# Householder steps of an on-chip eigensolver: z and y from one product, the rank-two update on 65 rows, and layer-0 work in 256-column pieces

## The chip, the cores and the metric

One core of one Trainium2 chip runs the whole program in one launch. The metric is device time in microseconds (us), the median of several runs. Engines are named as the profile names them: PE (TensorE, matrix products), DVE (VectorE), ACT (ScalarE), POOL (GpSimd), SP (SyncE, which issues the DMAs).

## What is computed

The input x is (128, 64, 256) in float32, with an adjacency matrix of 64 nodes. Four layers follow one another, each a layer norm, a ReLU, a graph layer, and an addition to x. Two of them matter here:

```python
# layer 0
agg = einsum('nm,bmd->bnd', A_hat, h)              # mix of the 64 nodes
h0  = relu(batchnorm(agg @ W1.T + b1))             # 256 -> 512
x   = x + batchnorm(h0 @ W2.T + b2)                # 512 -> 256
# layer 1
L_norm = d_inv_sqrt[:, None] * (diag(deg) - A) * d_inv_sqrt[None, :]
_, U = linalg.eigh(L_norm)                         # 64 x 64
agg = einsum('mn,bnd->bmd', U.T, h)
x   = x + einsum('nm,bmd->bnd', U, relu(agg @ W1 + b1) @ W2 + b2)
```

Layer 2 runs small LSTMs over windows, layer 3 is a graph attention. The eigenvectors of layer 1 depend only on the adjacency matrix, so they can be computed beside layer 0.

## The kernel before

The eigenvectors come from a chain of small, dependent steps; layer 0 is large and independent of them. `eigenvectors` (L1593) lays both into one order per engine. A `Plan` (L843) holds a model of time: each step has an engine, a `busy` time, a `ready` time after which its readers may start, and its needs. `chain` (L883) places a step of the eigensolver at once; before it does so, `fill` (L870) takes waiting steps of layer 0 (those given to `beside`, L889) into the gap ahead of it, as long as they end before the chain step's inputs are due plus a slack of the engine: 0.6 us for PE (T), 0.3 for ACT (S) and DVE (V). At most five PSUM banks of layer-0 results are open at a time. `emit` sorts all by planned time, and a helper (L799, the line that the profile gives for nearly every instruction) ties each instruction to the one before it on its engine. So the order on every engine is fixed when the program is built; nothing is reordered on the chip.

**The chain.** `tridiagonal` (L1003) reduces the 64x64 matrix `A` in 62 Householder steps, c = 63 down to 2, each by `householder` (L1041). A step holds the current row in every one of 64 partitions (`x`). Its norm comes from a Square with accumulation (ACT, `f_ja`), a Sqrt (`s0`), a reciprocal and a product on DVE (`r`, `tt`), and with the sign (`q`) gives the off-diagonal element `nb`. A small fix sets the reflector's entry, with `OA` holding a copy (on ACT) of an element of x. `KAP` is the reciprocal that scales the reflector, `uk` the scaled row (ACT). On PE two products make the rows z (one row of `A`, by a column of the identity) and y (a column of `A` times `A`), each broadcast to all partitions; ACT copies z from PSUM. DVE makes `uA` = z nb + y, a dot product `c2`, the row `v`, and from them the next step's row x in two instructions, ahead of the matrix itself. PE adds the two outer products of `uk` and `v` (contraction over one row), and DVE adds the result to `A`. Each row x is also sent to the matrix V by a DMA on SP; the row tiles x have eight buffers.

**The layer-0 work beside it.** 16 blocks of 512 rows. `hidden_block` (L1807): ReLU on ACT, per half of the features four 128x128 products with the mixing matrix into one PSUM bank (tile `ps`, one planned step), a copy on ACT, then 8 products of 512 columns, with statistics on DVE and a copy on ACT. `features0` (L1848), after batch-norm constants are known: ReLUs, 8 products of 512 columns per block, an output copy with a sum and a Square with a sum on ACT (tile `sums`). In float32 each product runs as two passes of the array.

**What follows.** After the last step the reflectors and the eigenvector computation proper (`fast.vectors`) run, with the rest of the planned layer-0 work. A verdict, `f_k_bad`, is summed by a PE product, and every engine reads it and branches over a slow path (L1617 and L1618). Then the constants of the second batch norm (`bn_b`, `bn_v`, `bn_r`, `bn_sh`) and the layer-1 inputs (`big`, ACT) are made.

Of the kernel before, what the change touches and what calls it, by code (L numbers as in the profile page):

```python
# [8 lines left out]
F32 = mybir.dt.float32  # L9
I32 = mybir.dt.int32  # L10
AF = mybir.ActivationFunctionType
ALU = mybir.AluOpType
# [772 lines left out]
GRID = 64  # L785

# [56 lines left out]
class Plan:  # L843
# [55 lines left out]

    def rest(self):  # L900

        while any(self.queue.values()):
            for e in self.queue:
                self.fill(e, 1e9)
# [8 lines left out]
class Fast:  # L913
# [31 lines left out]
    def sum(self, out, a, s, b, op0, op1=ALU.mult, name="junk"):  # L945

        w = a.shape[-1]
        j = self.t(f"{name}{a.shape[0]}", a.shape[0], 64)
        self.o.stt(j[:, 0:w], a, s, b, op0, op1, acc=out)
# [3 lines left out]
    def constants(self):  # L953
# [6 lines left out]
        self.P = t("P", 64, 1)  # L960
        iota(self.P[:], [[0, 1]], 0, 1)
# [21 lines left out]
        o.ts(self.low[:], self.J[:64, :], self.P[:], ALU.is_lt)  # L983
# [3 lines left out]
        o.copy(pi[:], self.P[:])  # L987
# [15 lines left out]
    def tridiagonal(self, S, made, plan):  # L1003

        o, nc, t = self.o, self.nc, self.t
        ident = self.k.ident
        A = self.A = t("A", 64, 64)
        m = t("SR", 64, 64)
        NB, OA, KAP, V = t("NB", 64, 64), t("OA", 64, 64, 2), t("KAP", 64, 64), t("V", 64, 64)
        nc.vector.memset(OA[:], 1.0)  # L1010
        for x in (KAP, NB, V):
            nc.vector.memset(x[:], 0.0)
        s0, r, tt, q, c2 = (t("h_" + x, 64, 1) for x in "s0 r t q c2".split())
        ja = t("ja", 64, 64)
        bc = lambda c, n=64: c.to_broadcast([n, 64])
        now = {}
        go = plan.chain

        def keep(name, a, b):
            now[name] = self.mm((a, b))  # L1020

        d = go("T", lambda: keep("p", S, self.JR[:]), [made], 0.3, 0.5)
        d = go("V", lambda: o.copy(m[:], now["p"][:]), [d], 0.15, 0.28)
        d = go("T", lambda: keep("p", self.JR[:], m[:]), [d], 0.3, 0.5)
        rest = go("V", lambda: o.copy(A[:], now["p"][:]), [d], 0.15, 0.28)
        d = go("T", lambda: keep("p", bc(ident[:64, 63:64]), A[:]), [rest], 0.3, 0.5)

        def first():
            x = now["x"] = self.rows.tile([64, 65], F32, name="f_x", bufs=8)
            o.copy(x[:, 0:63], now["p"][:, 0:63])  # L1030

        def square(w):
            x = now["x"]
            self.act(ja[:, 0:w], x[:, 0:w], AF.Square, accum_out=x[:, w:w + 1])

        row = go("V", first, [d], 0.15, 0.28)
        h = go("S", lambda: square(63), [row], 0.34, 0.42)
        for c in range(63, 1, -1):
            row, h, rest = self.householder(c, now, go, row, h, rest, (s0, r, tt, q, c2), square)

    def householder(self, c, now, go, row, h, rest, scalars, square):  # L1041

        o, nc, t = self.o, self.nc, self.t
        ident = self.k.ident
        A, NB, OA, KAP, V = self.A, t("NB", 64, 64), t("OA", 64, 64, 2), t("KAP", 64, 64), t("V", 64, 64)
        s0, r, tt, q, c2 = scalars
        bc = lambda a, n=64: a.to_broadcast([n, 64])
        x = lambda a, b: now["x"][:, a:b]
        nb = NB[:, c - 1:c]
        e, w = 0.001 * c, c - 1  # L1050

        def zy():
            now["zp"] = self.ps.tile([64, 64], F32, name="fps")
            nc.tensor.matmul(now["zp"][:, 0:c], bc(ident[0:c, c - 1:c], c), A[0:c, 0:c], start=True, stop=True)
            now["yp"] = self.ps.tile([64, 64], F32, name="fps")
            nc.tensor.matmul(now["yp"][:, 0:c], bc(A[0:c, c:c + 1], c), A[0:c, 0:c], start=True, stop=True)

        def row_z():
            now["z"] = self.rows.tile([64, 64], F32, name="f_z")
            self.act(now["z"][:, 0:c], now["zp"][:, 0:c], AF.Copy)  # L1060

        def row_uk():

            nc.sync.dma_start(V[c:c + 1, 0:c], now["x"][0:1, 0:c])
            now["uk"] = self.rows.tile([64, 64], F32, name="f_uk")
            self.act(now["uk"][:, 0:c], x(0, c), AF.Copy, scale=KAP[:, c:c + 1])

        def row_uA():
            now["uA"] = self.rows.tile([64, 64], F32, name="f_uA")
            o.stt(now["uA"][:, 0:c], now["z"][:, 0:c], nb, now["yp"][:, 0:c], ALU.mult, ALU.add)  # L1070

        def row_v():
            now["v"] = self.rows.tile([64, 64], F32, name="f_v")
            o.stt(now["v"][:, 0:c], x(0, c), c2[:], now["uA"][:, 0:c], ALU.mult, ALU.subtract)

        def outer():
            uk, v = now["uk"], now["v"]
            p = now["p"] = self.ps.tile([64, 64], F32, name="fps")
            nc.tensor.matmul(p[0:c, 0:c], uk[0:1, 0:c], v[0:1, 0:c], start=True, stop=False)
            nc.tensor.matmul(p[0:c, 0:c], v[0:1, 0:c], uk[0:1, 0:c], start=False, stop=True)  # L1080

        def row_x():
            now["x"] = self.rows.tile([64, 65], F32, name="f_x", bufs=8)
            o.stt(x(0, w), now["uk"][:, 0:w], now["v"][:, w:c], now["z"][:, 0:w], ALU.mult, ALU.add)

        z = go("T", zy, [rest], 0.34, 0.42)
        sq = go("S", lambda: self.act(s0[:], x(c, c + 1), AF.Sqrt), [h], 0.13, 0.23)
        oa = go("S", lambda: self.act(OA[:, c, 1:2], x(c - 1, c), AF.Copy), [row], 0.12, 0.22)
        zs = go("S", row_z, [z], 0.15, 0.26 + e)  # L1090
        sg = go("V", lambda: o.ts(q[:], x(c - 1, c), **halve(0)), [row])
        d = go("V", lambda: o.recip(r[:], s0[:]), [sq])
        d = go("V", lambda: o.stt(tt[:], r[:], x(c, c + 1), s0[:], ALU.mult, ALU.add), [d, h])
        b = go("V", lambda: o.mul(nb, q[:], tt[:]), [d, sg])
        d = go("V", lambda: o.stt(x(c - 1, c + 1), OA[:, c, :], nb, x(c - 1, c + 1), ALU.mult, ALU.add), [b, oa])
        d = go("V", lambda: o.recip(KAP[:, c:c + 1], x(c, c + 1)), [d])
        uk = go("S", row_uk, [d], 0.16, 0.32 + e)
        d = go("V", row_uA, [zs, b, z], 0.12 + e, 0.25 + e)
        d = go("V", lambda: self.sum(c2[:], now["uA"][:, 0:c], 0.5, now["uk"][:, 0:c], ALU.mult), [uk, d],
               0.2 + e, 0.28 + e)  # L1100
        v = go("V", row_v, [d], 0.15 + e, 0.26 + e)
        p = go("T", outer, [v], 0.25, 0.45)
        if c > 2:
            row = go("V", row_x, [v], 0.15 + e, 0.22 + e)
            row = go("V", lambda: o.stt(x(0, w), now["v"][:, 0:w], now["uk"][:, w:c], x(0, w), ALU.mult, ALU.add),
                     [row], 0.15 + e, 0.25 + e)
            h = go("S", lambda: square(w), [row], 0.28 + e, 0.36 + e)
        rest = go("V", lambda: o.add(A[0:c, 0:c], A[0:c, 0:c], now["p"][0:c, 0:c]), [p], 0.12 + e, 0.22 + e)
        return row, h, rest

    def reflectors(self):
# [8 lines left out]
        self.sum(kc[:], self.KAPs[:], 1.0, ident, ALU.mult)  # L1120
# [22 lines left out]
    def scale(self):  # L1143

        o, nc, t = self.o, self.nc, self.t
        NB, A = t("NB", 64, 64), self.A
        self.KAPs = t("KAP", 64, 64)
        DM, NE = t("DM", 64, 64), t("NE", 64, 64)
        o.mul(DM[:], A[:], self.k.ident[:64, :64])
        pe = self.mm((self.k.ident[:64, 1:2].to_broadcast([64, 64]), A[:]))  # L1150
# [315 lines left out]
class Kernel:  # L1466
# [126 lines left out]
    def eigenvectors(self):  # L1593
# [3 lines left out]
        with ExitStack() as ex:  # L1597
            fast = Fast(self.tc, ex, self)
            fast.constants()
            plan = Plan(dict(T=0.6, S=0.3, V=0.3), 5)  # L1600
# [206 lines left out]
    def hidden_block(self, i, r, m, plan, needs, used):  # L1807
# [9 lines left out]
        def mix(dc):  # L1817
            p = now["m", dc] = psum.tile([P, BT], F32, name="ps")
            for j in range(TPB):
                self.mm(p[:, j * P:(j + 1) * P], now["h"][:, j, dc * P:(dc + 1) * P], self.BDH[:])  # L1820

        def product(hc, kc):
            if kc == 0:
                now["p", hc] = psum.tile([P, BT], F32, name="ps")
            self.mm(now["p", hc][:], W1[:, kc, hc * P:(hc + 1) * P], now["z"][:, 2 + kc, :], kc == 0, kc == 1)
# [3 lines left out]
        for dc in range(2):  # L1829
            bank = []  # L1830
            x = beside("T", lambda dc=dc: mix(dc), h, 0.98, 1.1, bank)
# [4 lines left out]
        for hc in range(4):  # L1836
            bank = []
            x = beside("T", lambda hc=hc: product(hc, 0), mixed, 0.86, 0.9, bank)
            x = beside("T", lambda hc=hc: product(hc, 1), [x], 0.86, 1.0)
# [8 lines left out]
    def features0(self, plan, made, used):  # L1848
# [21 lines left out]
        for i in range(NB):  # L1870
# [15 lines left out]
            def product(oc, kc, i=i, now=now):  # L1886
                if kc == 0 and ("p", oc) not in now:
                    now["p", oc] = psum.tile([P, BT], F32, name="ps")
                self.mm(now["p", oc][:], W2[:, kc, oc * P:(oc + 1) * P], now["z"][:, kc, :], kc == 0, kc == 3)
# [11 lines left out]
            for oc in range(2):  # L1901
# [4 lines left out]
                for kc in range(4):  # L1906
                    x = beside("T", lambda oc=oc, kc=kc, f=product: f(oc, kc), [z[kc]] + ([x] if x else []), 0.86, 1.0,
                               None if kc or x else bank)
# [878 lines left out]
```

## Time and profile before

| | |
|---|---|
| median of 3 runs | 2329.3 us (2326.33 to 2331.57) |
| profiled execution, span | 2325.1 us |
| first outer product of the chain | 14.87 us |
| last update of A | 272.2 us |
| verdict product (f_k_bad) on PE | 364.35 us |
| PE goes on after the branch | 370.16 us |
| layer-1 inputs begin on ACT | 372.03 us |
| mean interval of outer products (61 of them) | 4.2 us |

The profile is one execution on the chip. Its page gives the busy time of each engine; the busy time can be had for any stretch of the span, and a timeline lists instructions one after the other with start, length, engine, operation, the output and the inputs by tile names, the array's rows and columns in use (128*128 for a full product) and the shape. Consecutive alike instructions are merged (x6: six passes). PE's passes overlap, so the distance between two starts says more than the length of one. In brackets stand idle time ahead of an instruction and what ended it. Of the span the first 372 us, less than a sixth, hold all that the change touches; layers 1 to 3 after it are the same in both kernels.

### The profile page before, as it was taken

Reading aid. Unit: us, or ns where it says so; the run is one execution under the profiler, and the core shown is the slowest. Engines: PE = TensorE matmul, PEld = TensorE weight load, DVE = VectorE, ACT = ScalarE, POOL = GpSimd, SP = SyncE. Lnnn points to the kernel's source line nnn. Section 1 sums busy time; section 2 is a strip of 40 time slices with the busy share of each in tenths; the row PEclk is TensorE's granted clock in tenths of the full one; section 3 lists DMA queues with packets and bytes.
Section 4 is the critical chain, followed back from the end, with each engine's and each line's share of the span. In section 5 each row is a group of like instructions: output and inputs, shape, how many; then the busy total and the mean of one; then the engine's idle time right before and its main releaser. Section 6 shows DMA issues by size and latency. Waiting matters only on the chain.

```text
span 2325.1 us, 32725 instructions
## 1 busy us (share of the span) xinstructions
PE 2283.6 (98%) x12169; PEld 1633.1 (70%) x12169; DVE 1629.3 (70%) x4054; ACT 1139.5 (49%) x2483; POOL 3.0 (0%) x26
## 2 busy tenths in 40 slices
PE   7999998999999999999999999999999999999999
PEld 4554445676777788888999998888885544554544
DVE  8887676888447777666767676559756686766667
ACT  5765865754436654433444444336435544444321
POOL 0000000000000000000000000000000000000000
PEclk9999999999999999999999999999999999999999
DMA  5000211230000000001000002000010000000001
GB/s 171 1 1 26 65 56 30 71 83 19 1 37 0 1 19 1 1 1 37 1 1 1 1 1 73 1 1 17 1 46 28 1 5 15 15 19 14 14 24 46
DMA packets 61065, 54.81 MB, mean 24 GB/s; under 512 B 15203, under 2 KB 58724, under 8 KB 60900
## 3 DMA queue, kind: packets, MB, share of 16 engines
q1 hardware_dynamic: 60900, 52.66, 7.4%
q8 instruction: 97, 1.59, 0.3%
q14 instruction: 68, 0.56, 0.1%
HBM read 35.86 MB, written 16.78 MB: 23 GB/s over the span
## 4 chain that ended last, share of the span: by engine, by line
PE 79%; DVE 3%; issue 1%; ACT 1%; DMA 0%; SPq 0%; ACTq 0%; DVEq 0%
PE ps L799 69%; PE acc L799 5%; PE pt L799 4%; PE pe L799 1%; PE y L799 1%; DVE aw L799 1%; DVE X L799 1%; DVE sm_m L799 0%; DVE XV L799 0%; ACT ls_g L799 0%; ACT h L799 0%; DVE ls_g L799 0%; ACT big L799 0%; DVE ls_t L799 0%; DVE sm_e L799 0%
## 5 line engine op out<-in xcount | busy, mean ns | idle before, releaser
L799 ACT ACTIVATE ls_g<-ls_g,ls_b 128x512 f32<-128x512 f32 (+4 forms) x472 | 243.1, 565 | 151.4 <-DVE ls_g L799 149.6
L799 ACT ACTIVATE ls_g<-ps,ls_b 128x256 f32<-128x256 f32 (+3 forms) x268 | 115.5, 470 | 330.9 <-PE ps L799 327.7
L799 PE MATMUL ps<-z,w 128*128 128x512 f32 x512 | 254.9, 621 | 0.9 <-ACT z L799 0.9
L799 PE MATMUL ps<-big,X 128*128 128x176 f32 (+3 forms) x848 | 212.7, 366 | 0.1
L799 DVE TENSOR_TENSOR ls_g<-ls_z,ps 128x512 f32<-128x512 f32 (+5 forms) x256 | 146.8, 579 | 91.9 <-PE ps L799 90.4
L799 DVE TENSOR_TENSOR aw<-at,ed_OST 128x1024 f32<-128x1024 f32 x128 | 149.9, 1219 | 83.0 <-PE ps L799 82.8
L799 PE MATMUL ps<-ls_tx,X 128*128 128x160 f32 (+2 forms) x960 | 206.8, 326 | 0.6 <-ACT ls_g L799 0.6
L799 PE MATMUL ps<-X,X 128*128 128x160 f32 (+1 forms) x896 | 199.1, 306 | 0.0
L799 PE MATMUL ps<-X,ls_w 128*128 128x256 f32 x640 | 190.5, 379 | 0.0
L799 PEld LDWEIGHTS ps<-ls_tx,X 128*128 128x128 f32 x960 | 161.8, 190 | 15.1 <-DVE X L799 4.8
L799 PEld LDWEIGHTS ps<-big,X 128*128 128x128 f32 x848 | 145.9, 190 | 29.7 <-issue 19.4
L799 DVE TENSOR_TENSOR X<-ls_g 128x1024 f32<-128x1024 f32 (+2 forms) x108 | 117.4, 1087 | 49.9 <-ACT ls_g L799 49.8
L799 ACT ACTIVATE r<-ps 128x512 f32<-128x512 f32 x256 | 131.6, 614 | 41.5 <-PE ps L799 41.4
L799 PEld LDWEIGHTS ps<-X,X 128*128 128x128 f32 x896 | 148.4, 190 | 0.0
L799 PE MATMUL ps<-X,ls_s 128*128 128x256 f32 x480 | 142.3, 379 | 0.0
L799 PEld LDWEIGHTS ps<-z,w 128*128 128x128 f32 x512 | 87.2, 190 | 69.0 <-issue 60.2
L799 PE MATMUL ps<-ls_tx,ls_s 128*128 128x256 f32 x464 | 134.8, 379 | 0.0
L799 PE MATMUL ps<-ed_S,Q 64*128 64x512 f32 x512 | 132.9, 618 | 1.4 <-DVE hT L799 0.7
L799 PE MATMUL ps<-ls_tx,ls_w 128*128 128x256 f32 x464 | 133.2, 380 | 0.0
L799 PEld LDWEIGHTS ps<-X,ls_w 128*128 128x128 f32 x640 | 121.4, 190 | 16.8 <-DVE X L799 0.3
L799 PE MATMUL ps<-big,ls_w 128*128 128x256 f32 x464 | 131.9, 379 | 0.7 <-ACT ls_z L799 0.7
L799 PE MATMUL ps<-aw,ed_ODT 128*64 128x512 f32 x512 | 117.3, 595 | 0.1
(545 smaller groups left out, 4019.0 us busy)
## 6 DMA issues: line engine op xcount, KB each, us to landing
X<-in_x_dram SPq DMA_DIRECT2D x32, 512.0 KB
xs<-X SPq DMA_DIRECT2D x16, 512.0 KB
X<-xs SPq DMA_DIRECT2D x16, 512.0 KB
out_dram<-X SPq DMA_DIRECT2D x31, 256.0 KB
X<-in_L_gnn_Wih_t_dram SPq DMA_DIRECT2D x4, 512.0 KB
ls_w<-in_L_gnn_Wih_t_dram SPq DMA_DIRECT2D x4, 512.0 KB
ls_w<-in_L_gnn_Whh_t_dram SPq DMA_DIRECT2D x4, 512.0 KB
w<-in_L_gnn_W_t_dram SPq DMA_DIRECT2D x2, 512.0 KB
```

The lines of the kernel that those rows point to most:

```text
L799: i = method(*a, **kw)
```

## The change

1. Rows z and y come from one product `zy`: the weights are a tile `EX` of 65 rows with 128 columns, 64 of a unit vector (made by ACT, one step and more ahead, `unit`) and 64 of a masked row for y. The result has z in the partitions 0 to 63 and y in 64 to 127 of one PSUM tile; `uA` reads y from the upper half.
2. The masked row `m` for the next y is made by DVE from the outer products' PSUM tile and the old `A`, ahead of the update of `A`.
3. The two outer products run on tiles `L` and `R` of 65 rows and 65 columns, zero but for the row wanted; v is written into R by DVE, the row of L by one more ACT copy (`side`).
4. `nb` is computed as r qh + qs, with `qs` on ACT beside the reciprocal on DVE; the dot product (`dd`) takes x in place of uk. The copy into `OA` moves from ACT to POOL. The x tiles have six buffers.
5. Layer-0 products are issued in halves of 256 columns, the mixes in pairs, each a planned step of its own.
6. `weigh` lays each Householder step with 27 choices of the slacks, scores each by the layer-0 work that it takes in, less 2.7 times its end, and keeps the best.

The order of instructions of the two kernels shows the same layer-0 work, 151,040 columns of products in all. Ahead of the last outer product lie 98,048 of them (109,568 before), between it and the verdict product 38,656 (41,472), and after the verdict product, ahead of PE's read of the branch, 14,336 (none before). With these, one Square of `features0` on ACT and nine small instructions of the second batch norm on DVE move behind the branch.

The core of the diff:

```diff
+    def weigh(self, make, slacks, worth, cost):
+
+        free, queue = dict(self.free), {e: list(v) for e, v in self.queue.items()}
+        n, k = len(self.steps), len(self.opened)
+        best = None
+        for slack in [*slacks, None]:
+            self.slack = slack or best[1]
+            made = make()
+            if slack is None:
+                return made
+            gain = sum(x.busy * worth.get(x.engine, 0.0) for x in self.steps[n:])
+            gain -= cost * max(x.at + x.ready for x in made)
...
+        self.slacks = [dict(T=a, S=b, V=v, P=0.0) for a in (0.2, 0.45, 0.8) for b in (0.1, 0.3, 0.6) for v in (0.1, 0.35, 0.65)]
...
         for c in range(63, 1, -1):
-            row, h, rest = self.householder(c, now, go, row, h, rest, (s0, r, tt, q, c2), square)
+            row, h, rest = plan.weigh(lambda: self.householder(c, now, go, row, h, rest),
+                                      self.slacks, dict(T=1.0, S=0.5, V=2.0), 2.7)
+
+    def unit(self, c):
+        self.act(self.ex[c % 2][0:64, 0, :], self.k.ident[0:64, c - 1:c].to_broadcast([64, 64]), AF.Copy)
...
-        def zy():
-            now["zp"] = self.ps.tile([64, 64], F32, name="fps")
-            nc.tensor.matmul(now["zp"][:, 0:c], bc(ident[0:c, c - 1:c], c), A[0:c, 0:c], start=True, stop=True)
-            now["yp"] = self.ps.tile([64, 64], F32, name="fps")
-            nc.tensor.matmul(now["yp"][:, 0:c], bc(A[0:c, c:c + 1], c), A[0:c, 0:c], start=True, stop=True)
+        def products():
+            zy = now["zy"] = self.ps.tile([P, 64], F32, name="fps")
+            nc.tensor.matmul(zy[:, 0:c], ex[c % 2][:].rearrange("p a b -> p (a b)"), A[:, 0:c], start=True, stop=True)
...
         def outer():
-            uk, v = now["uk"], now["v"]
-            p = now["p"] = self.ps.tile([64, 64], F32, name="fps")
-            nc.tensor.matmul(p[0:c, 0:c], uk[0:1, 0:c], v[0:1, 0:c], start=True, stop=False)
-            nc.tensor.matmul(p[0:c, 0:c], v[0:1, 0:c], uk[0:1, 0:c], start=False, stop=True)
+            p = now["p"] = self.ps.tile([P, 64], F32, name="fps")[:R]
+            nc.tensor.matmul(p[:, 0:c], left[:, 0:R], right[:, 0:c], start=True, stop=False)
+            nc.tensor.matmul(p[:, 0:c], right[:, 0:R], left[:, 0:c], start=False, stop=True)
...
+        zy = go("T", products, [rest], 0.25, 0.45)
+        sq = go("S", lambda: self.act(s0[:], x(c, c + 1), AF.Sqrt), [h], 0.13, 0.25)
+        oa = go("P", lambda: nc.gpsimd.tensor_copy(OA[:, c, 1:2], x(c - 1, c)), [row], 0.2, 0.4)
+        sg = go("V", lambda: o.ts(q[:], x(c - 1, c), **halve(0)), [row], 0.09, 0.25)
+        g = go("V", lambda: o.mul(qh[:], q[:], x(c, c + 1)), [sg, h], 0.09, 0.25)
+        d = go("V", lambda: o.recip(r[:], s0[:]), [sq], 0.09, 0.25)
+        qr = go("S", lambda: self.act(qs[:], s0[:], AF.Copy, scale=q[:]), [sq, sg], 0.13, 0.25)
+        zs = go("S", row_z, [zy], 0.14, 0.27 + e)
+        b = go("V", lambda: o.stt(nb, r[:], qh[:], qs[:], ALU.mult, ALU.add), [d, g, qr], 0.09, 0.25)
...
+        uA = go("V", row_uA, [b, zy, zs], 0.12 + e, 0.25 + e)
+        k = go("V", lambda: o.recip(kap, x(c, c + 1)), [d], 0.09, 0.25)
+        uk = go("S", row_uk, [k], 0.16, 0.32 + e)
+        sides = [go("S", lambda: side(left[0:1, 0:c], now["x", c], KAP[0:1, c:c + 1]), [k], 0.14, 0.27 + e)]
+        d = go("V", lambda: self.sum(dd[:], now["uA"][:, 0:c], 0.5, x(0, c), ALU.mult), [uA], 0.2 + e, 0.28 + e)
+        v = go("V", lambda: o.stt(right[0:64, 0:c], now["uk"][:, 0:c], dd[:], now["uA"][:, 0:c], ALU.mult, ALU.subtract),
+               [d, uk], 0.12 + e, 0.26 + e)
+        p = go("T", outer, [v] + sides, 0.5, 0.7)
...
+            m = go("V", lambda: o.stt(ex[w % 2][0:64, 1, :], now["p"][0:64, w:c].to_broadcast([64, 64]), A[0:64, w:c],
+                                         self.MK[:, w:c].to_broadcast([64, 64]), ALU.add, ALU.mult), [p], 0.12, 0.25)
         rest = go("V", lambda: o.add(A[0:c, 0:c], A[0:c, 0:c], now["p"][0:c, 0:c]), [p], 0.12 + e, 0.22 + e)
+        if c > 3:
+            go("S", lambda: self.unit(c - 2), [zy], 0.14, 0.3)
         return row, h, rest
...
-            x = beside("T", lambda hc=hc: product(hc, 0), mixed, 0.86, 0.9, bank)
-            x = beside("T", lambda hc=hc: product(hc, 1), [x], 0.86, 1.0)
+            x = beside("T", lambda hc=hc: product(hc, 0, 0), mixed, 0.43, 0.43, bank)
+            for k, kc in ((0, 1), (1, 0), (1, 1)):
+                x = beside("T", lambda hc=hc, k=k, kc=kc: product(hc, k, kc), [x], 0.43, 0.6 if k and kc else 0.43)
```

## The prediction, made before the changed kernel had run

> **What bounds the kernel now.** I read the page first, then the busy time by stage, then the timeline of TensorE (PE) in one late step, then the timeline around the branch.
>
> ```profile
> span 2325.1 us, 32725 instructions
> ...
> PE 2283.6 (98%) x12169; PEld 1633.1 (70%) x12169; DVE 1629.3 (70%) x4054; ACT 1139.5 (49%) x2483; POOL 3.0 (0%) x26
> ```
>
> ```profile
> core 0: us, PE busy (x) PEld busy (x) DVE busy (x) ACT busy (x) POOL busy (x), PEclk, DMA share, GB/s
> 11.00:272.30 261.30, 251.43 (x1165) 130.96 (x1166) 195.85 (x1015) 179.08 (x610) 0.00 (x0) 0.99 0.15 45
> 272.30:364.40 92.10, 89.35 (x302) 39.97 (x302) 70.53 (x338) 55.51 (x140) 0.00 (x0) 1.00 0.16 46
> 364.40:374.00 9.60, 4.06 (x24) 3.92 (x24) 2.66 (x18) 3.53 (x8) 0.74 (x3) 0.82 0.25 72
> ```
>
> PE is busy 98% of the span, and the edit touches only what lies ahead of 374 us. The first window is the Householder chain with layer 0 beside it (fill), the second the eigenvector chain with the rest of the fill, the third the branch. PE is busy in 251 of 261 us, at full clock, so the first window is short of PE. But "busy" hides what a step costs:
>
> ```profile
> 222.18 0.21 PE L799 MATMUL fps<-f_v,f_uk 1*15 1x15 f32 x2
> 222.24 0.20 PE L799 MATMUL fps<-f_uk,f_v 1*15 1x15 f32 x2
> 222.37 1.13 PE L799 MATMUL ps<-z,w 128*128 128x512 f32 x2
> 223.42 0.28 PE L799 MATMUL fps<-f_A,ident 14*64 14x14 f32 x2
> 223.56 0.26 PE L799 MATMUL fps<-f_A 14*64 14x14 f32 x2
> 223.75 2.84 PE L799 MATMUL ps<-z,w 128*128 128x512 f32 x6
> 226.53 0.21 PE L799 MATMUL fps<-f_v,f_uk 1*14 1x14 f32 x2
> ```
>
> One step, from outer product to outer product, takes 226.53-222.18 = 4.35 us. A 512-column pass that follows its like starts every 0.429 us. The two passes here take 223.42-222.37 = 1.05 (0.19 over their 0.858), the six take 2.78 (0.21 over 2.574). In the trace that excess is always 94 ns when the array's form changes from 128*128 to a small one, and 104 ns on the first pass back; between products of one form it is 2 ns (1433 cases). So the step is 8 x 0.429 = 3.43 fill, 0.19 outer, 0.33 rows z and y, 0.40 for four changes of form: 0.92 fixed. It has no room for more.
>
> **The step's PE price.** New: one product for z and y (65 rows, 128 weight columns), two outer products on 65x65. The layer-0 mixes, whose weights and moving data are both 128 columns, start every 111 ns; zy is two such passes, 0.22. The outer passes have 65 columns of weights; rows z and y above, with 64, started every 58 ns, so 3 x 0.058 + 0.107 for the last, after which the fill loads 128 columns again: 0.28. Sum 0.50. Whether the 0.40 goes is the open point. The nearest rows speak against it: products with 64 rows by 128 columns pay 90 to 98 ns when they follow the full form, and 65 rows occur nowhere in the trace. The Trainium skill ("TensorEngine Tiling (Array Packing)", Tiling Modes and Key Properties) has array forms only of 32, 64 or 128 rows or columns and says that switching the mode drains the array; 65 fits none but the full one. By the row a step keeps the 0.40, zy and the outer products cost what rows z and y do above, 0.34 and 0.33, and the price is 1.07; by the rule 0.50. I take 0.50, with 1.07 as the other end.
>
> **Fill.** Layer 0 is the same 151,040 columns of fill, in pieces of 256 instead of 512: 0.215 us start to start against 0.429, so nothing. The order of instructions puts 98,048 columns ahead of the last outer product (109,568 before), 164.3 us for 183.6: 2.64 per step for 2.95. With 0.50 PE owes 194.5 us in the 61 steps (with 1.07: 229). Before, by the same count, it owed 247 (each step at least its chain) and the trace has 257.1.
>
> **The step's chain.** With PE relieved, the row's own loop sets the floor. From the trace's shortest hops, the loop before is 3.06 us (x1 0.26, x2 0.19 to its Square, sqrt 0.34, and on by twelve hops to v). The new one: x1 0.27, x2 0.28, Square 0.24, sqrt 0.34, root to NB 0.46 (reciprocal and qs side by side), fix 0.25, KAP 0.25, uk 0.19, v 0.36 = 2.64; t, one multiply and c2's wait for uk are out of it. Beside it VectorE (DVE) has 13 chain instructions for 12 and ScalarE (ACT) 7 for 5 (side, qs and the unit column come, OA goes), about +0.14 and +0.2 us per step. DVE's busy share rises to some 75%; fill ahead of a chain instruction already costs up to 0.45 per step (medians lie that far over the shortest hops). An added wait: m, the masked row for the next y, and the A update stand on DVE ahead of q, qh, r and NB, and wait for the outer product. Here A's update began 0.66 us after v's end; q to NB are needed some 1.1 us after it, so it costs nothing unless PE comes over 0.4 late. I put the floor at 3.0 to 3.3 with this noise. Step by step, the larger of floor and PE's debt gives 215 to 225 over 61 steps. Like before, something comes on top: the first steps have little fill ready and an unwarmed clock (3.5), the row buffers go from 8 to 6, so that one row (near 35 us) waits for a V-row transfer behind the X loads on SP (first V transfer lands near 37.5: 2.5), the bn1 turn (about 2). I take 227 us, 3.72 per step, bounds 214 and 245: **30 us saved** (12 to 43).
>
> **OA's copy on GpSimd (POOL).** ACT loses 0.19 x 62. POOL is empty here; its nearest row, an IOTA of 128x4, is 0.15 us. The copy is needed by fix only 1.04 us later (Square, sqrt, root to NB), so by the rows it costs nothing. The Trainium skill ("SBUF — State Buffer", on the shared port pair) says that GpSimd and a VectorE operation with two SBUF inputs lock each other out for a whole instruction. By that rule one DVE operation per step may be held 0.13 to 0.15: 62 x 0.13 = 8 us. No row here shows POOL beside DVE; I take 0, with 0 to +8 inside the bounds. A gain is excluded beyond ACT's share, counted above.
>
> **Set-up.** Six memsets on POOL (rows of 0.09 to 0.13 each) end near 4 us, the mask and unit columns are one or two instructions each, used at 11 us or later: nothing; without that cover 1 us.
>
> **Tail and branch.**
>
> ```profile
> 364.35 0.27 PE L799 MATMUL fps<-f_k_bad,ones 64*64 64x1 f32 x2
> ...
> 370.16 3.11 PE L799 MATMUL ps<-ones,ident 128*128 128x128 f32 x13 [5.54 <-DVEq L1618]
> ...
> 372.03 1.52 ACT L799 ACTIVATE big<-big,bn_sh,bn_sc 128x512 f32<-128x512 f32 x2 [1.41 <-DVE bn_sh L799]
> ```
>
> Before, all fill lies ahead of the k_bad product, and PE stands 5.54 us until the branch is read. In the new order 38,656 columns (64.8 us) lie between the last outer product and k_bad, for 41,472 (69.5). Of these 4.7 us I count 1.5, as the eigenvector chain needs its own time in those 92 us (bounds 0 and 4.7). And 56 products of 256 columns, 56 x 0.429 = **24.0 us**, come after k_bad, with nothing beside them, ahead of PE's own read of the branch. They can't hide under its 5.5 us: PE reads after them. One ACT square and nine small DVE steps move behind the branch; the layer-1 inputs started 7.63 us after the last fill, I get 7.9: +0.3 (bounds -3.5, if DVE and ACT are through the branch early, and +2).
>
> **The sum.** -30 - 1.5 + 24.0 + 0.3 = -7.2. The profiled execution has 2325.1 us of span, 4.2 below the median of 2329.3 and just under the lowest run; I apply the difference to the median: **2322 us**. So most of what the chain saves is fill that it no longer covers.
>
> **The rivals.**
> 1. *Slower.* The 65-row products change the array's form after all, a fixed price of 1.07 per step. PE's debt is then 229, with floors and starts 245: -12 - 1.5 + 24.3 = +11, about 2340. For it: the rows at 64 rows. Against: the rule. It decides where the steps take 239 us (+4.7): on the line between (0.50, 227) and (1.07, 245), a fixed price of 0.88.
> 2. *No difference.* DVE and ACT, with three more chain instructions and all of their fill, delay the row by 0.7 instead of 0.4 (floor 3.35): 234 us, and the sum is -0.3. For it: DVE is at 75% before and loses its slack. Against: finer pieces and layouts chosen per step from 27 slacks.
> 3. *Faster still.* The chosen layouts keep the floor at 2.8: 211 + 8 = 219 to 220 us, net -14.5, 2315; or the branch is read under the fill, -3.5. For it: the shortest steps of before reach their floor.
> 4. *It isn't done as said*: the order shows it is (fill counts, three products per step), so no more than in rival 1.
>
> **How the numbers follow.** A measurement of this kernel tells about 0.2% (4.7 us) from no change. Forecast (-5 to -11) 0.39, rival 3 (beyond -11) 0.18, rival 2 0.26, rival 1 0.17. Faster 0.57, same 0.26, slower 0.17. The range reaches into rival 3 to a net of -21 and into rival 1 to its +11: 2308 to 2340.
>
> **What would show it.** In the new profile: fill passes next to chain products start 0.43 after their double passes without the 94 and 104 ns (else rival 1); last A update near 242 us (at 250 or later, nothing is gained); k_bad near 333, the end of fill near 357, PE again near 362; POOL with 62 copies well under 1 us each; one row waiting on a transfer near 35 us. I am wrong if DVE's waits for ACT and ACT's for DVE grow past 0.5 us per step, or if PE is idle for more than some 35 us of the first window.

## The result, and the profile after

The changed kernel takes 2355.0 us (2354.7 to 2356.2, 4 runs) against 2330.4 (2326.3 to 2331.7, 4 runs): 1.0117 times as long, 95% interval 1.0102 to 1.0133. I had forecast 2322 us and given slower a chance of 0.17. Its profiled execution has 2354.3 us of span, 29.2 more than that of before. In the same order as for before, first the page, then the busy time by stage (the ends of the windows are the last update of A, the verdict product and the start of layer 1):

```profile
span 2354.3 us, 33968 instructions
...
PE 2287.2 (97%) x12557; PEld 1742.8 (74%) x12557; DVE 1644.0 (70%) x4118; ACT 1167.5 (50%) x2608; POOL 14.6 (1%) x94
```

```profile
11.00:282.70 271.70, 234.87 (x1301) 193.72 (x1302) 209.74 (x1077) 190.09 (x697) 10.99 (x62) 0.94 0.13 36
282.70:372.40 89.70, 86.29 (x442) 66.05 (x441) 70.59 (x338) 55.22 (x136) 0.00 (x0) 1.00 0.20 59
372.40:401.60 29.20, 26.65 (x131) 23.20 (x130) 2.76 (x18) 17.40 (x46) 0.00 (x0) 1.00 0.18 57
```

The columns are length, then busy time of PE, PE's weight loads, DVE, ACT and POOL, granted clock, DMA share and GB/s. The chain's window got 10 us longer instead of 30 shorter. PE, busy for 251 of 261 us before, is busy for 235 of 272 here, at 0.94 of its clock for 0.99; DVE and ACT are busier. The third window was 9.6 us long before; new in it are 24 us of layer-0 products with no chain beside them.

PE at the same time as in the prediction's excerpt; the chain is at c = 18 and 17 here, where it was at 15 and 14 before:

```profile
222.26 0.26 PE L800 MATMUL fps<-f_R,f_L 65*65 65x18 f32 x2 [0.22 <-DVE f_R L800]
222.37 0.27 PE L800 MATMUL fps<-f_L,f_R 65*65 65x18 f32 x2
222.49 1.11 PE L800 MATMUL ps<-z,w 128*128 128x256 f32 x4
223.93 0.37 PE L800 MATMUL fps<-f_A,f_EX 65*128 65x17 f32 x2 [0.32 <-DVE f_h_q L800]
224.14 1.97 PE L800 MATMUL ps<-z,w 128*128 128x256 f32 x8
225.95 0.24 PE L800 MATMUL fps<-f_R,f_L 65*65 65x17 f32 x2
```

Twelve passes of 256 columns are 2.6 us of work, and the step takes 3.69: PE waits ahead of both chain products, for v (the tile R) and for the new A. The eight passes from 224.14 to 225.95 take 1.81, only 0.08 over 8 x 0.216: the change of form has gone. What PE waits for is on DVE:

```profile
222.42 0.23 DVE L800 SCALAR_TENSOR_TENSOR f_x<-f_R,f_uk,f_x 64x17 f32<-64x17 f32 x1
222.71 0.70 DVE L800 BATCH_NORM_STATS2 st<-ps 128x6 f32<-128x512 f32 x1
223.32 0.26 DVE L800 SCALAR_TENSOR_TENSOR f_EX<-fps,f_A,f_MK 64x64 f32<-64x64 f32 x1
223.62 0.16 DVE L800 TENSOR_TENSOR f_A<-f_A,fps 18x18 f32<-18x18 f32 x1
223.71 0.13 DVE L800 TENSOR_SCALAR f_h_q<-f_x 64x1 f32<-64x1 f32 x1
```

The outer products had started at 222.26, but m begins at 223.32: a layer-0 statistic of 0.70 us stands ahead of it, behind m the update of A, and behind that q, without which ACT can't make qs. The waits of PE in the window of the steps, all rows above 2 us, in us in total, times, longest; first before (11 to 272.3), then after (11 to 282.7):

```profile
PE fps L799 <- DVE f_v L799: 3.7, 4, 1.4
PE fps L799 <- DVE m_m L799: 3.0, 2, 2.4
```

```profile
PE fps L800 <- DVE f_h_q L800: 16.0, 24, 2.0
PE fps L800 <- DVE f_R L800: 12.9, 18, 2.0
```

q has nothing to do with zy; it is DVE's next instruction when zy's true input, A, arrives. PE's 7 us of waits on the chain became 29.

Stage by stage, against before: first outer product 14.34 us (-0.5); the 61 intervals 267.9 for 257.1 (**+10.8**); last outer product to verdict 90.1 for 92.4 (-2.3); verdict to layer-1 inputs 29.2 for 7.7 (**+21.5**: 24.4 of layer-0 products, and 2.9 less for the branch: the verdict is 25 us old when PE comes to it, and PE stands 2.2 us instead of 5.5). Sum +29.5; the rest of the kernel takes 0.4 less.

### The profile page after: what moved, and what is told of

It is laid out like the page before. It is cut to its first block, busy times and chain, and to the rows that moved or that the text cites. A ratio compares the mean times of both kernels' runs of the same rounds, so it can differ in the third digit from the quotient of the medians.

```text
span 2354.3 us, 33968 instructions
## 1 busy us (share of the span) xinstructions
PE 2287.2 (97%) x12557; PEld 1742.8 (74%) x12557; DVE 1644.0 (70%) x4118; ACT 1167.5 (50%) x2608; POOL 14.6 (1%) x94
## 4 chain that ended last, share of the span: by engine, by line
PE 78%; DVE 3%; ACT 1%; issue 1%; DMA 0%; ACTq 0%; DVEq 0%; SPq 0%
PE ps L800 68%; PE acc L800 5%; PE pt L800 4%; PE pe L800 1%; PE y L800 1%; DVE aw L800 1%; DVE X L800 0%; DVE sm_m L800 0%; DVE XV L800 0%; ACT ls_g L800 0%; ACT h L800 0%; DMA ls_w<-in_L_gnn_Wih_t_dram 0%; DVE ls_g L800 0%; DMA ed_a<-in_L_gnn_a_dram 0%; ACT big L800 0%
## 5 line engine op out<-in xcount | busy, mean ns | idle before, releaser
L800 PE MATMUL ps<-z,w 128*128 128x256 f32 x1024 | 265.1, 404 | 1.3 <-ACT z L800 1.2
L800 PEld LDWEIGHTS ps<-z,w 128*128 128x128 f32 x1024 | 191.9, 198 | 27.8 <-ACT z L800 3.4
L800 DVE TENSOR_TENSOR ls_g<-ls_z,ps 128x512 f32<-128x512 f32 (+5 forms) x256 | 146.9, 579 | 91.7 <-PE ps L800 90.1
L800 ACT ACTIVATE big<-ps 128x512 f32<-128x512 f32 x96 | 68.7, 747 | 100.1 <-PE ps L800 91.7
```

Of the source, the lines that this page charges most:

```text
L800: i = method(*a, **kw)
```

## The experiments

From this profile I held two theories: Q, that layer-0 instructions on DVE and ACT stand in the new chain's way, and O, that the chain's own new order makes it wait. Others (W, L, C) came with later results. Every chip time stands beside runs of before on the same chip. The table has what the traces show; columns are layer-0 products, counted without 3,584 columns of unread products that `features0` starts with.

| kernel | ratio to before (95%) | 61 intervals, us | columns ahead of the last outer product | after the verdict | layer-1 inputs, us |
|---|---|---|---|---|---|
| before | 1 | 257.1 | 105,984 | 0 | 372.0 |
| changed | 1.0117 (1.0102 to 1.0133) | 267.9 | 94,464 | 14,336 | 401.6 |
| plain_layout | 1.0411 (1.0394 to 1.0428) | 231.0 | 37,888 | 62,976 | 466.8 |
| rows_64 | 1.0135 (1.0116 to 1.0154) | 268.3 | 94,464 | 14,336 | 402.0 |
| order_kap_q | 1.0107 (1.0085 to 1.0129) | 272.1 | 94,720 | 14,080 | 405.5 |
| thin_stats_after | 1.0157 (1.0141 to 1.0174) | 235.3 | 77,696 | 34,048 | 405.4 |
| thin_stats_before | 0.9999 (0.9990 to 1.0009) | 256.1 | 103,424 | 3,072 | 375.2 |
| pieces_before | 1.0022 (1.0014 to 1.0030) | 254.8 | 101,376 | 7,424 | 378.9 |
| outer65_before | 0.9960 (0.9946 to 0.9973) | 253.6 | 109,056 | 0 | 365.6 |
| all65_before | 1.0141 (1.0125 to 1.0156) | 241.9 | 76,800 | 30,720 | 410.4 |
| unit_on_pool | 1.0110 (1.0094 to 1.0125) | 265.2 | 96,512 | 12,288 | 397.4 |
| pieces512_after | 0.9995 (0.9986 to 1.0004) | 257.5 | 106,496 | 0 | 371.4 |
| ahead24 | 1.0052 (1.0038 to 1.0066) | 261.7 | 100,352 | 8,448 | 388.0 |
| unread_products | 1.0121 (1.0105 to 1.0137) | 268.6 | 94,208 | 14,336 | 402.6 |
| all65_weighed | 0.9985 (0.9978 to 0.9993) | 254.6 | 108,544 | 0 | 367.1 |
| order_512 | 1.0007 (0.9998 to 1.0015) | 266.4 | 109,568 | 0 | 376.4 |
| pieces_before_ahead24 | 1.0003 (0.9996 to 1.0011) | 259.1 | 106,496 | 2,048 | 376.5 |
| outer65_ahead24 | 0.9973 (0.9964 to 0.9981) | 249.3 | 105,984 | 0 | 365.7 |

**The chain by itself.** Both kernels with the layer-0 work held back:

```diff
     def fill(self, engine, until):
-        while True:
+        while not getattr(self, "held", False):
...
         zy = go("T", products, [rest], 0.25, 0.45)
+        go("T", lambda: warm(5), [zy], 1.1, 1.1)
...
+        go("T", lambda: warm(2), [v], 0.44, 0.44)
```

> The kernel before with all layer-0 work held back until the Householder steps are over; in its place PE runs two products of 128x64 after each outer product and five after rows z and y, which nobody reads, so that it stays busy. The total is long and means nothing; only the interval of the steps counts. It was 4.20 us on average with the layer-0 work beside it. Both theories: 3.1 to 3.4 us, the chain's own length (its shortest steps took 3.06).

> The changed kernel in the same way: layer-0 work held back, unread products on PE in its place, no choice of layouts. Its interval was 4.37 us on average with the layer-0 work. Theory Q (competition): the new chain by itself is as short as the prediction's sum, 2.6 to 2.9 us, and is stretched by layer-0 instructions that stand ahead of it on DVE and ACT. Theory O (its own order): m and the update of A ahead of q, qh, r and NB, and uA ahead of KAP, make the chain wait for the outer product and for z by itself; it is no shorter than that of before, 3.1 to 3.4 us.

The intervals were 4.33 and 3.93 us, and neither is the chain's length. The products meant to keep PE awake got in the way: in each run all 744 pairs of their passes started 213 ns or more apart, where the same product takes 112 in a later run, so five of them (ten passes) held PE for some 2.2 us and the outer product waited for them (it started a median of 1.57 us after v in the one, 0.95 in the other). Nothing follows from these two.

The next run gave the chain's length by chance. It drops the choice of layouts:

```diff
-            row, h, rest = plan.weigh(lambda: self.householder(c, now, go, row, h, rest),
-                                      self.slacks, dict(T=1.0, S=0.5, V=2.0), 2.7)
+            row, h, rest = self.householder(c, now, go, row, h, rest)
```

> The changed kernel without the choice among 27 layouts: every step with the slacks of before (0.6, 0.3, 0.3). Theory W (the choice of layouts is what costs: it lets layer-0 work in ahead of the chain because it values DVE's work at 2.0): the steps fall to 4.0 us or less and the total to 2340 or less. Theories Q and O: the layouts matter little, 2345 to 2365.

2423.5 us, outside all three. With the slacks of before, next to no layer-0 work is laid into the new chain's middle steps, and 62,976 columns are left to the end. By the planner's own times the new chain is dense: on DVE and ACT it seems to leave few gaps into which an instruction of 0.6 us fits with a slack of 0.3. A window of such steps, the columns as above:

```profile
55.00:165.00 110.00, 41.00 (x198) 33.48 (x198) 79.56 (x465) 54.70 (x269) 5.85 (x33) 0.50 0.01 1
```

Nearly empty of layer-0 work, DVE is still busy 72% of the time, and the 34 steps without a layer-0 instruction on DVE take 3.34 us on average, with PE at half its clock. At full clock the shortest step of the changed kernel takes 2.97. My sum of hops was 2.64: it took fix to KAP as 0.25 (0.42 here, because uA stands between), and the root to NB as 0.46 (0.77, because r waits behind m, A, q and qh).

**Is PE still the bound?**

```diff
-R = 65
+R = 64
```

> The changed kernel with 64 rows in place of 65 in the three products of a step, so that the array changes its form again (four changes, 0.4 us a step). If PE still bounds the steps, as in my sum, the steps get longer by all of it: +24 us, about 2379. If the chain on DVE and ACT bounds them, most of it disappears in PE's idle time: +0 to +10, 2355 to 2365.

2357.7 us, 2.7 above the changed kernel (1.0135 times before, for 1.0117): the changes of form are back on PE and the intervals stay (268.3 for 267.9). PE's price no longer bounds the steps. The same from the other side, with more work on PE in the same order:

```diff
             nc.tensor.matmul(zy[:, 0:c], ex[c % 2][:].rearrange("p a b -> p (a b)"), A[:, 0:c], start=True, stop=True)
+            p = self.psv.tile([P, 64], F32, name="fvps")
+            for _ in range(2):
+                self.k.mm(p[:], self.k.ident[:], self.k.ones[:, 0:64])
```

> The changed kernel, its order untouched, with two products of 128x64 more after each zy, which nobody reads (0.4 us of PE a step at full clock). Theory C (PE, idle in a seventh of the steps' time, loses its clock: 81 of 921 layer-0 passes ran at half speed, for 24 of 665 with pieces of 512): with more to do it keeps its clock, and the kernel gets no slower or even up to 8 us faster, 2347 to 2355. Without that mechanism the added work costs 0.3 to 0.9 of its own time: +8 to +24, 2363 to 2380.

2358.1 us: some 27 us of products (4 passes of 112 ns, 61 times) cost 3. In the one profile of each, passes at or near half speed fell from 81 of 921 to 46 of 922, and the time that they lose from 11.8 to 6.0 us. So some clock is lost where PE idles, but giving back half of it won nothing: it is not the 28 us, and the theory's own forecast was a little too good.

**The chain's order and DVE's room.** Two instructions placed earlier:

```diff
-        uA = go("V", row_uA, [b, zy, zs], 0.12 + e, 0.25 + e)
         k = go("V", lambda: o.recip(kap, x(c, c + 1)), [d], 0.09, 0.25)
+        uA = go("V", row_uA, [b, zy, zs], 0.12 + e, 0.25 + e)
...
+            sg = go("V", lambda: o.ts(q[:], nx(w - 1, w), **halve(0)), [row], 0.09, 0.25)
```

> The changed kernel with two instructions of its chain placed earlier on DVE: KAP ahead of uA, and q right after the new row, ahead of m and of the update of A. Theory O (the chain waits for its own instructions): KAP no longer waits behind uA (0.17 us) and qs on ACT no longer waits for q (up to 0.3 us), so the steps fall by 0.2 to 0.4 us and the total to 2330 to 2345. Theory Q (layer-0 work ahead of the chain on DVE and ACT): the time lost goes to other waits, 2348 to 2358.

2355.0 us, as the changed kernel. The hops did shorten (medians: fix to KAP 0.42 to 0.25, root to qs 0.32 to 0.22), and the intervals did not (272.1, in an execution 6 us above the median): the time went to other hops (means: NB to fix rose from 0.37 to 0.47, the outer product to m from 0.88 to 0.94). Theory O falls. Once more, where pieces are large (below):

> The changed kernel with 512-column pieces and with KAP ahead of uA and q ahead of m. With 256-column pieces this order moved the time by nothing. Theory O would have 0.2 us a step come out here, where little else is lost: 2312 to 2320. Theory Q: the step is full of DVE and ACT work and nothing comes out, 2323 to 2333.

2331.4 us against 2327.0 without it: no gain either.

Statistics on 32 of 512 columns, in both kernels (the batch norm's constants change with it):

```diff
-            bank.append(beside("V", lambda hc=hc: nc.vector.bn_stats(self.st1[:, hc, i, :], now["p", hc][:]), [x],
-                               0.62, 0.7, urgent=i >= NB - 2))
+            bank.append(beside("V", lambda hc=hc: nc.vector.bn_stats(self.st1[:, hc, i, :], now["p", hc][:, 0:32]), [x],
+                               0.14, 0.25, urgent=i >= NB - 2))
```

> The changed kernel with the hidden blocks' statistics on DVE taken over 32 of 512 columns (64 instructions of 0.70 us become some 0.2), which changes the batch norm's constants; all else is kept. Theory Q: DVE's room is what the new chain lacks; the steps fall from 4.37 to 4.0 us or less and the total by 20 us or more. Theory O: the order inside the chain costs it, the steps fall by less than 0.15 us, the total by less than 10.

> The kernel before with the same thin statistics. Its steps are bound by PE, so by both theories they gain little, 0 to 10 us of 2328; a gain as large as in the changed kernel would say that DVE's room bounds both alike.

Before stays (2328.6; steps 4.20 for 4.22): DVE's room is not its bound. In the changed kernel the steps fall from 4.39 to 3.86, and yet the total rises to 2364.0: with less DVE work to score, the choice of layouts took shorter steps with 77,696 columns, and 34,048 were left to the end. So the run does not test theory Q: the layout moved too, and the 16,768 columns that left the steps are 28 us of PE's work, against 33 us that the intervals lost.

Two readings of the kept traces speak to Q. The first is a correlation. Over the last 58 steps a step of before fits 1.2 to 1.7 us + 0.8 to 0.9 x its layer-0 time on PE; one of the changed kernel fits 2.0 to 2.3 us + 0.4 to 0.5 x the layer-0 time on DVE + 0.4 to 0.65 x that on ACT + 0.1 to 0.3 x that on PE (the ranges come from different ways to count PE's time).

The second goes back from the last outer product to the first, at each instruction to what released it or, where it did not wait, to the one before it on its engine. In the changed kernel this path of 268 us has 84 to 98 us of layer-0 instructions on DVE and ACT, 104 to 116 of the chain's own on these two, 49 to 58 on PE (by where one draws the line for a wait), and the hand-overs. With 512-column pieces (below) it is much the same: 89 to 98 of layer-0 work on DVE and ACT, and 42 to 52 on PE. In before, PE alone has 115 to 215 of the 257, and layer-0 work on DVE and ACT 23 to 72. So some 1.5 us of each new step are layer-0 instructions on DVE and ACT that the chain stands behind.

One of the chain's ACT instructions, moved to GpSimd:

```diff
-        self.act(self.ex[c % 2][0:64, 0, :], self.k.ident[0:64, c - 1:c].to_broadcast([64, 64]), AF.Copy)
+        self.nc.gpsimd.tensor_copy(self.ex[c % 2][0:64, 0, :], self.k.ident[0:64, c - 1:c].to_broadcast([64, 64]))
```

> The changed kernel with the unit column for z made by GpSimd in place of ACT (0.24 us a step off ACT). Theory Q (DVE and ACT are what the steps now lack): the fit over its steps gives 0.38 us of step for each us on ACT, so -0.1 x 61 = -6 us, 2345 to 2352. Theory O: no difference, 2353 to 2357. If GpSimd's larger copy blocks DVE: 2357 to 2370.

2355.8 us: no difference in the medians, though in the profile layer 1 starts 4 us earlier. Inconclusive at this size.

**The pieces.** Each kernel with the pieces of the other:

```diff
-            x = beside("T", lambda hc=hc: product(hc, 0), mixed, 0.86, 0.9, bank)
-            x = beside("T", lambda hc=hc: product(hc, 1), [x], 0.86, 1.0)
+            x = beside("T", lambda hc=hc: product(hc, 0, 0), mixed, 0.43, 0.43, bank)
+            for k, kc in ((0, 1), (1, 0), (1, 1)):
+                x = beside("T", lambda hc=hc, k=k, kc=kc: product(hc, k, kc), [x], 0.43, 0.6 if k and kc else 0.43)
```

> The kernel before with the layer-0 products in pieces of 256 columns and the mixes in pairs, and nothing else changed. My sum put the pieces at nothing: 2323 to 2333. If the pieces cost PE time by themselves (weights loaded twice as often), 5 to 15 us more.

> The changed kernel with layer-0 products of 512 columns again, layouts still chosen. By the run of before with 256-column pieces (+5 us) the pieces cost a little; with the choice of layouts they may also have been what it needed. Pieces as such at fault: 2345 to 2352. Pieces needed by the new layouts: 2358 to 2380.

Before with small pieces: 2334.5, +5. The changed kernel with 512-column pieces: **2327.0, no different from before**. So the small pieces carry nearly the whole loss, which no theory had; the new chain with large ones has the intervals of before to 0.4 us, with PE far less busy (237 of 261 us for 251):

```profile
11.00:272.20 261.20, 236.83 (x1043) 131.26 (x1044) 209.55 (x1077) 204.53 (x731) 10.99 (x62) 1.00 0.16 45
```

Why should pieces matter that cost PE nothing? `fill` looks at the first 12 waiting steps of an engine, and 12 steps are half as much work when the pieces are halved:

```diff
-            for x in self.queue[engine][:12]:
+            for x in self.queue[engine][:24]:
```

> The changed kernel, with fill looking at the first 24 waiting steps of an engine in place of 12 (L874), and nothing else. The halved pieces make 12 steps of PE only six products of 512 columns; theory L: this is why less layer-0 work was laid beside the chain (94,464 columns for 106,496 with pieces of 512). The program's own order then takes in 11 us more of it ahead of the last outer product, at 3 us more of chain: 2342 to 2349. If the loss is not in what is laid where, but in what PE's idle time does to it on the chip: 2350 to 2358.

> The kernel before with 256-column pieces and a look-ahead of 24 steps. Its pieces alone cost 5 us, with 7,424 columns left after the verdict product. If the look-ahead is the whole of that (theory L), the order takes in as much layer-0 work as before and the time is that of before: 2325 to 2332. If the pieces cost by themselves, 2333 to 2338.

2341.8: half of the loss gone with this one number, as theory L had it. With the old chain all of it goes: 2328.9, no different from before.

```profile
11.00:276.50 265.50, 235.91 (x1347) 192.27 (x1348) 210.08 (x1077) 194.47 (x708) 11.05 (x62) 0.99 0.14 40
```

PE's clock is at 0.99 again. The 15 us that still part this from 2327.0 are about what the 8,448 columns still left after the verdict take (14.2 us, at 0.43 for 256); why the choice of layouts leaves them with small pieces even so, no run settles.

**PE's saving where PE is the bound.** Parts of the change in the kernel before:

```diff
+        side = go("S", lambda: self.act(left[0:1, 0:c], x(0, c)[0:1], AF.Copy, scale=KAP[0:1, c:c + 1]), [k], 0.14, 0.27 + e)
...
-            nc.tensor.matmul(p[0:c, 0:c], uk[0:1, 0:c], v[0:1, 0:c], start=True, stop=False)
-            nc.tensor.matmul(p[0:c, 0:c], v[0:1, 0:c], uk[0:1, 0:c], start=False, stop=True)
+            nc.tensor.matmul(p[:, 0:c], left[:, 0:R], right[:, 0:c], start=True, stop=False)
+            nc.tensor.matmul(p[:, 0:c], right[:, 0:R], left[:, 0:c], start=False, stop=True)
```

> The kernel before with one part of the change alone: the two outer products on tiles of 65 rows and columns, with one more ACT copy a step (side); order, layouts and everything else as before. PE loses two of four changes of the array's form (0.2 us a step) and pays 0.28 for 0.19 of outer products. If PE bounds the steps of before (0.9 us of step for each us of PE, as its steps show), and the added ACT copy does not: -0.1 x 61 = -6 us or so, 2320 to 2326. If ACT's copy lengthens the chain (0.29 x 61 at the most): 2330 to 2345.

2321.7, faster by 0.40% (0.27 to 0.54): -8 for an expected -6. Not all of it is PE's price, for the planner lays this kernel anew too: in the profile layer 1 starts 6.4 us earlier, of which 3.5 lie in the intervals (with 3,072 columns, 5.2 us of PE's work, more in them) and 2.0 behind the verdict, where more of the second batch norm now stands ahead of the branch. Now z and y too:

```diff
+        rest = go("V", lambda: o.mul(self.yc[0:64], A[0:64, c:c + 1], self.MK[:, c:c + 1]), [rest], 0.09, 0.22)
...
-            nc.tensor.matmul(now["yp"][:, 0:c], bc(A[0:c, c:c + 1], c), A[0:c, 0:c], start=True, stop=True)
+            nc.tensor.matmul(now["yp"][:, 0:c], self.yc[:].to_broadcast([R, R]), A[:, 0:c], start=True, stop=True)
```

> The kernel before with the outer products and the two products for z and y on 65 rows, by a masked column (one small DVE multiply a step) and the side copy on ACT; the order, the recurrence for NB, the layouts and 512-column pieces stay. All four changes of form go (0.40), the products cost 0.28 + 0.28 for 0.19 + 0.33. PE-bound steps: -0.36 x 0.9 x 61 = -20 us at the most, 2310 to 2322, less what one DVE and one ACT instruction more give back. If those two give back all of it: 2326 to 2340. This tells whether the saving on PE is real where PE is the bound.

2364.1, a miss: its steps are shorter than those of before (241.9 us), but with one instruction more on DVE and one on ACT the fixed slacks found room for less, and 30,720 columns were left over. With the choice of layouts in it (cost 3.0):

> The run with all products of before on 65 rows had 30,720 columns left after the verdict product, for none before: its one instruction more on DVE closed the gaps that the fixed slacks look for. Here it has the choice among 27 layouts (cost 3.0 in place of 2.7), with 512-column pieces, so that about as much layer-0 work lies beside the chain as before. If the loss of 34 us was what was laid where: 2318 to 2332. If the added DVE and ACT instructions lengthen the chain on the chip: 2340 or more.

2325.2: the 34 us had been the layout. The version that the runs point to, outer products on 65 rows and the longer look-ahead:

> The kernel before with the outer products on 65 rows (2321.7 us so far) and a look-ahead of 24, 512-column pieces: the order then ends the chain 2 us earlier with 4 us less layer-0 work in it. 2317 to 2323; the look-ahead has little to give where pieces are large.

2320.9, faster than before by 0.27% (0.19 to 0.36), and within the error of the same without the look-ahead. These two are the only clear gains over both kernels, beside all65_weighed's 0.15%.

## Why the prediction was wrong

- **Right:** the 65-row products don't change the array's form (a pass ahead of one takes 0 to 1 ns over its like, for 94). The first pass after one still pays 84 ns, for 104, so that part was no change of form. The chain's price on PE is 0.43 + 0.17 = 0.60 a step, for 0.50 foreseen and 0.92 before: a saving of 0.32 instead of 0.42. Where PE bounds, part of it shows (outer65_before).
- **Right:** tail -2.3 (foreseen -1.5), layer-0 products after the verdict +24.4 (24.0). The branch, -2.9, lies inside the bounds of -3.5 and +2, though +0.3 was the number. POOL's copies take 0.18 us and end at least 1 us ahead of fix; m, a DVE operation with two SBUF inputs, took a median of 0.275 us beside a copy and 0.260 without one (30 and 31 cases), so that nothing like the 8 us of the shared port came.
- **The step that failed:** "Step by step, the larger of floor and PE's debt gives 215 to 225", and from it 227 us for the 61 intervals; 267.9 were measured, 41 more, and that is more than the whole error of the total (33); the branch gave 3 of it back. The larger of the two would hold if layer-0 work were only PE's. Each part of it also brings its DVE and ACT instructions (some 1.3 and 1.8 us of each step, of 3.4 and 3.1 that these engines are busy in all), which stand in the queues among the chain's own. I counted them as noise, 0.4 us on a floor of 2.64; on the path above they are some 1.5. A step is floor and a good part of these together. With 512-column pieces that alone gives 257.5: all of the 30 us saved on paper is given back, and the other 10 of the 41 come with the small pieces. That PE and the chain's own order don't bound the new steps was tried by experiment; that DVE's and ACT's layer-0 instructions do was read from the traces, since no run took them out of the same layout.
- **A reading that could have told:** "DVE's busy share rises to some 75%". It was 75% already (195.85 of 261.30 in the first row of the windows). The 209.7 us that DVE was busy in the changed kernel's window would have filled 91% of a window of the length foreseen. Both signs named for being wrong came: ACT's waits for DVE grew from 0.50 to 0.85 us a step, past 0.5, and PE was idle for 37 us of the first window, past 35.
- **The second miss:** "Layer 0 is the same 151,040 columns of fill, in pieces of 256 instead of 512: 0.215 us start to start against 0.429, so nothing". On PE that is so. But the pieces are also the planner's units, and with its look-ahead of 12 it laid less work (94,464 columns for 106,496) beside a chain that took longer (267.9 us for 257.5). The pieces with the new layouts cost 28 us, of which 13 go with the look-ahead alone. I had the result of this in hand, 98,048 columns for 109,568, and took it to mean shorter steps, where it meant idle PE.
- **The rivals.** The second named the mechanism (three more chain instructions, DVE without slack), but gave it 7 us over the 61 intervals (234 for 227), not 41. The first had the right sign for a reason that the trace refutes.

## What to carry to other kernels

When an engine that is the bound is relieved, don't stop at the next latency chain: add up what every engine in the chain has to issue per step, chain and companion work together, and ask whether the gaps of the new chain still take the companion's instructions. A planner with a limit counted in its own units (here a look-ahead in steps) is part of the kernel: cut its units in half, and the limit is halved too. Here the part that saved on the bound and added little elsewhere, the outer products, was worth more alone than with the rest.

## What the runs showed of the hardware

- In the changed kernel's chain window, where PE is busy for 86% of the time at a granted clock of 0.94, 81 of 921 layer-0 passes ran at or near half speed (11.8 us lost). It is 33 of 662 (4.4 us, 0.99) in the kernel before with 96% busy, and 24 of 665 (2.1 us, 1.00) in pieces512_after with 91%.
- PE busy all the time is no full speed either. In chain_after it was fed with passes of 64 columns; here are ten of the unread ones, and what comes after them:

```profile
151.14 2.37 PE L800 MATMUL fvps<-ones,ident 128*128 128x64 f32 x10
153.31 0.37 PE L800 MATMUL fps<-f_R,f_L 65*65 65x30 f32 x2
```

They start 213 ns apart (2.17 us for ten). The same product among passes of 256 columns, in unread_products, takes 112:

```profile
152.79 0.64 PE L800 MATMUL fvps<-ones,ident 128*128 128x64 f32 x4
153.26 4.10 PE L800 MATMUL ps<-z,w 128*128 128x256 f32 x18
```

The chain's own passes take twice as long too (the second outer product's start 111 ns apart for 59), so it is PE's speed and not this product.

The clock column of the windows does not show it:

```profile
100.00:180.00 80.00, 80.00 (x415) 80.00 (x416) 49.85 (x294) 32.83 (x164) 3.57 (x20) 1.00 0.01 1
```

PE and its weight loads are busy for 80 of 80 us there at a granted clock of 1.00. But the first clock record in this trace is the rise to full speed at 357.9 us, and the column counts the time ahead of the first record as 1.00. Before it, 128-column passes start 213 ns apart, after it 112. In the kernel before that rise stands at 21.7 us, behind 16 passes of 128 columns, with 213 ns ahead of it and 112 after it. So PE ran at half speed through all Householder steps of chain_after, busy as it was; what would have raised its clock there, no run tells. The distance of starts is the safer reading.
